# A four-layer convolution and state-space network on one core: its projections repacked as 128 + 64 columns, and the hand-planned instruction order made again with other costs

## The chip, the cores and the metric

The kernel runs on one core of a Trainium2 chip. A core has five engines that run side by side and meet only through semaphores: TensorE (PE, matrix products; its loads of stationary weights have a row of their own, PEld), VectorE (DVE), ScalarE (ACT), GpSimd (POOL) and SyncE (SP, which here only issues copies). Copies between the DRAM tensors and the on-chip tiles are carried out by 16 DMA engines that all queues share. The metric is the time of one execution in microseconds (us), lower is better: 9278.05 us is the median of three runs of the kernel before (9277.84, 9278.05 and 9299.97).

## What is computed

Sixty-four images of 96 channels and 28 x 28 pixels, all in float32, pass four layers. Layer 0 is an inverted residual block whose depthwise kernels and projection weights are mixed for each image out of four experts; layers 1 and 3 are plain inverted residual blocks; layer 2 is a selective state-space block on the four quarters of the image. The expansion goes from 96 to 576 channels, the projection back to 96.

```
# layer 0                                  (per image: rw = softmax weights of 4 experts)
out = silu(bn1(exp_w @ x))                 # 96 -> 576
out = silu(bn2(depthwise 5x5 (out, kern))) # kern = mix of 4 experts' kernels
out = out * sigmoid(squeeze-excite(out))
x   = x + bn3((mix of 4 experts' pw_w) @ out)   # 576 -> 96, the projection
# layers 1 and 3
out = relu(bn1(w1 @ x)); out = relu(bn2(depthwise 3x3 (out, wd)))
x   = x + bn3(w3 @ out)                    # 576 -> 96, the projection
# layer 2, for each quarter of the image
b = silu(dwconv3x3(p2(h))); b = four directional scans of b (16 states a channel); y = norm(b) * silu(p1(h))
x = x + y * gate(y)
```

## The kernel before, in words

All 64 images run through one program without loops; images are software-pipelined. In the slot of image t the scans of layer 2 run for image t (`mamba`, `scans`, `head`, `tail`), beside them the depthwise layers 1 of image t+1, 0 of image t+2 and 3 of image t-1 (`convs`), and the expansion of the next job.

**A convolution layer** has three parts. `expand` (L735, L765) multiplies the image with the expansion weights in eight products of 128 output channels by 392 pixels and one last pair of 64 channels; ACT takes each out of PSUM into a bordered tile (L719), and the ACT queue stores it in a DRAM tensor `ex` (L752, L778). `load` fetches it back on the SP queue into `rep`, each channel in several shifted rows (L791 with three copies for layer 0, L798 with four copies for layers 1 and 3), and fetches or builds the tap weights `wd` (L825 from DRAM, L598 on POOL). `depthwise` (L851) convolves: stationary weights of 32 columns in four column groups of the PE array, layer 0 with 96 rows, layers 1 and 3 with 64 rows and so two row groups at once; ACT takes each result into an `acc` tile (L861). There are nine `acc` tiles to a layer. A lane of `rep` and `acc` holds a channel together with the parity of the row, so that the 392 columns of an `acc` tile are half an image.

**The projection** (`project`) is what the change repacks. An `acc` tile g has 128 lanes: 64 channels, each for even rows (o = 0) and odd rows (o = 1). For each g and each parity one matmul with 96 output channels adds to one of two PSUM banks, with weights that are zero at the lanes of the other parity. That is 18 matmuls of 128 rows, 96 columns and 392 pixels a layer (L888). In float32 each of them is two records in the profile, and each record has its own weight load. Then DVE adds bank o and the bias to the rows of parity o of the image (L892, two instructions). For layer 0 the weights are made for each image: PE mixes the experts (L985), DVE multiplies in the gates (L1010, four instructions, 480 or 384 elements wide).

**The scans**: DVE multiplies (L1307) and scans forwards and backwards (L1312, L1317), POOL combines (L1264), ACT makes the decays (L1285) and copies `du` (L1295), PE collects (L1239).

**The order** of every engine's instructions is written by a planner, `Plan`. Each operation is entered with its engine, an assumed cost in us, what it reads and writes, and a due time: the slot's start `T * t` plus an offset, plus a correction from the table `DUE` for its kind. `Plan.run` then plays the program through with these assumed costs and issues, engine by engine, the operation that is ready and due first. On the chip only the order is kept; no due time is enforced. The planner knows which ACT function table is loaded (a change costs `TABLE`), and where it expects PE to lie idle it puts in products of zeros (L549, `idle`). Two things of it matter here: an operation is never issued more than `AHEAD` us before it is due, and a copy was assumed to arrive after its issue plus `land` (or a size by a rate) plus `LAND`. The copies' semaphores are eight in number and are handed out in turn, SP and ACT together: a copy waits until the one eight places earlier in the program has landed.

Of the kernel before, what the change touches and what calls it, by code (L numbers as in the profile page):

```python
# [15 lines left out]
P = 128  # L16
# [148 lines left out]
def pack_l1(ins, layer):  # L165
# [12 lines left out]
    out = np.zeros((4, 2, CB, 2, NG, C), np.float32)  # L178
    for o in range(2):
        out[:, o, :, o] = w3.reshape(4, 2, CB, NG, C)[:, o]  # L180
    p.add("w3", out.reshape(P, 2 * NG, C))
# [4 lines left out]
def pack_l2(ins):  # L186
# [41 lines left out]
PE, ACT, DVE, POOL, SP = "PE", "ACT", "DVE", "POOL", "SP"  # L228
EXP, PLUS, SILU = "exp", "plus", "silu"
# [11 lines left out]
    71, -2, 48, -17, 58, 181, 21, -12, 9, -37, -2, 21, 37, -23, 1, -16, 19, -12, 30, -17, 33, -40, 12, -8, -30, -60,  # L241
    -12, 9, 0, -16, 16, -56, 115, 47, -23, -9, 16, 45, -29, 63, -28, 34, 12, 35, 43, 2, -32, -7, 21, -7, 6, 14, 37,
    13, -22, 36, -19, 13, -27, 7, -23, -17, 130, -19, 113, 50, 16, 35, 28, 2, 22, 11, -45, 12, -30, 30, -30, -13, -6,
    -6, -12, -8, -7, 20, 24, 117, 11, 25, -20, 15, -13, 1, 51, 43, 29, 147, 47, 40, -10, -15, -7, 10, 30, -10, 20,
    129, 8, 11, 31,
# [17 lines left out]
class Plan:  # L263
# [4 lines left out]
    AHEAD = 45.0  # L268

    HOP = {PE: 1.0, DVE: 0.6, ACT: 0.4, POOL: 0.4, SP: 0.2}  # L270
    LAND = 0.7
    ALONE = 130e3
    RATE = 300e3
    TABLE = 1.28
    ANY_ORDER = ("ps", "gs")
    WARM, WINDOW = 0.7, 3.4
    GRACE = {PE: 0.3, ACT: 0.2, DVE: 0.25, POOL: 0.25, SP: 0.0}
# [10 lines left out]
    def op(self, engine, cost, fn, r=(), w=(), due=None, table=None, nbytes=0, after=(), land=None, lock=False):  # L288
        o = Op()
        o.engine, o.cost, o.fn, o.table, o.nbytes = engine, cost, fn, table, nbytes  # L290
        o.land, o.lock = land, lock or engine == POOL
        kind = self.k.kinds.setdefault((fn.__code__, self.tag), len(self.k.kinds))
        o.due = (self.due if due is None else due) + (DUE[kind] if kind < len(DUE) else 0.0)
# [39 lines left out]
    def run(self, start=0.0):  # L333
# [3 lines left out]
        table, dma, left, lock, ahead = None, start, len(self.ops), start, None  # L337
        used = []
# [18 lines left out]
        while left:  # L357
            best = None
            for e, q in queue.items():
                cands = []  # L360
                for o in q:
                    t = max(free[e], o.ready, o.due - self.AHEAD)
                    if o.lock:
                        t = max(t, lock)
                    if best and t > best[0] + 1.0:
                        continue
                    if o.allocs:
                        p = place(o)
                        if p is None:
                            continue  # L370
                        t = max(t, p)
                    cands.append((t, o))
# [3 lines left out]
                key = lambda c: (c[1].due + (8.0 if c[1].table and c[1].table != table else 0.0), c[1].n)  # L376
# [9 lines left out]
            if o.table and o.table != table:  # L386
                cost += self.TABLE
                table = o.table
            o.fill = 0.0
            if e == PE:  # L390
# [7 lines left out]
                used.append((t - o.fill, t + cost))  # L398
            free[e] = end = t + cost
            o.behind = None  # L400
# [7 lines left out]
            if o.nbytes:  # L408

                dma = max(dma, t + 0.5) + o.nbytes / self.RATE  # L410
                end = max(dma + 1.5, t + cost + (o.land or 2.0 + o.nbytes / self.ALONE)) + self.LAND
# [6 lines left out]
            for b in set(o.bufs):  # L418
                b.left -= 1
                b.end = max(b.end, end + 0.2)  # L420
            for d, data in o.out:
                d.wait -= 1
                if data:
                    d.ready = max(d.ready, end + (self.HOP[d.engine] if d.engine != e or o.nbytes else 0.0))
# [58 lines left out]
class Kernel:  # L483
    T = 145.0
# [13 lines left out]
        wp=(1, [P, 2, NG, C]),  # L498
# [90 lines left out]
    def fold_bn3(self, row, w3):  # L589

        k = w3.shape[1]
        self.nc.vector.tensor_tensor(w3, w3, row.rearrange("p (a o) -> p a o", a=1).to_broadcast([P, k, C]), ALU.mult)
# [12 lines left out]
    def setup(self, fold, banks):  # L605
# [22 lines left out]
        for layer, c in ((1, c1), (3, c3)):  # L628
# [4 lines left out]
            self.fold_bn3(self.row_of(banks, s3, eye, f"fold_row{layer}"), c("w3"))  # L633
# [75 lines left out]
    def expand(self, d):  # L709
# [17 lines left out]
        for t in range(4):  # L727
# [3 lines left out]
            for h in range(2):  # L731
                ps = pl.buf("ps")

                def mm(ps=ps, t=t, h=h):
# [4 lines left out]
                pl.op(PE, 0.72, mm, r=d["keys"], w=[ps], after=[("pad", i, h)])  # L739
                pl.op(  # L740
                    ACT, 0.68, lambda ps=ps, t=t, h=h, pad=pad: evict(pad[:, :, 1 + 7 * h : 8 + 7 * h, 2:30], ps, t),
# [4 lines left out]
            def send(t=t, pad=pad):  # L746
# [8 lines left out]
                ACT, 0.35, send,  # L755
                r=[("pad", i, 0), ("pad", i, 1)], w=[("ex", d["exkey"], t)], nbytes=524288, land=3.5,
# [23 lines left out]
        pl.op(PE, 0.81, mm, r=d["keys"], w=[ps], after=["hpad"])  # L780
        pl.op(ACT, 0.68, lambda: evict(pad[:, :, :, 2:30], ps, 4), r=[ps], w=["hpad"], table=d["table"])
        pl.op(ACT, 0.7, store, r=["hpad"], w=[("ex", d["exkey"], 4)], nbytes=230000, land=3.2)
# [19 lines left out]
    def load(self, d, u):  # L802
# [8 lines left out]
            SP, 0.32 * n, lambda: self.rows(d, rep, ch, sets),  # L811
            r=[("ex", d["exkey"], ch // P)], w=[rep], nbytes=n * CB * 4 * 1792, land=4.2 if sets == 2 else 2.8,
# [8 lines left out]
        if layer == 0:  # L821
            pl.op(POOL, 1.3, spread, r=[d["kern"]], w=[wd])
        else:
            pl.op(
                SP, 0.55, lambda: nc.sync.dma_start(wd()[:lanes, :TAPS], self.taps[layer][u][:lanes]),  # L825
                w=[wd], nbytes=lanes * TAPS * 4,
# [3 lines left out]
    def depthwise(self, d, u):  # L830
# [34 lines left out]
        pl.op(PE, 0.69 * k, mm, r=[rep, wd], w=[*banks, *accs])  # L865
        for h, (ps, acc) in enumerate(zip(banks, accs)):
            pl.op(
                ACT, 0.88 if sums else 0.68, lambda ps=ps, acc=acc, h=h: evict(ps, u if sums else 2 * u + h, acc),
# [3 lines left out]
    def project(self, d):  # L872
# [3 lines left out]
        if d["layer"] == 0:  # L876
            wp = self.squeeze_excite(d)
            terms = lambda o, g: (wp()[:, o, g], accs[g]())
        else:
            w3, wp = d["c"]("w3"), "none"  # L880
# [655 lines left out]
```

## Time and profile before

| what | before |
|---|---|
| median of 3 runs | 9278.05 us |
| the profiled execution | 9292.98 us (its span 9291.2 us) |
| granted TensorE clock, mean | 0.967 |
| PE, DVE, POOL, ACT busy | 96%, 84%, 73%, 68% of the span |
| products of zeros (L549) | 150 records, 71.6 us |
| ACT table loads, all lines | 1077 instructions in the program, 1283 ns each |
| all copies | 2030 MB, 218 GB/s, DMA engines 71% busy in mean |

The profile shows one execution. Its page gives each engine's busy time, groups of instructions by source line with their mean duration, and the idle time of the engine just before them with what ended it. A "busy" PE is a rough reading, since matmul records overlap each other; the distance from the start of one row of the timeline to the start of the next is the better measure of what a stretch of matmuls takes. The granted clock is the share of TensorE's full clock that was let through.

Once the pipeline is full, the images follow each other evenly. The routing product of layer 0 (L921) comes once an image; from its start at 555.84 us to that at 8897.88 us there are 59 images, 141.4 us each.

### The profile page before, as it was taken

The page shows a single profiled execution, that of the slowest core. Times are in us where ns is not written, and L with a number is a line of the kernel's source. Part 1 is how long each engine was busy: PE and PEld are TensorE (multiplying, and loading weights), DVE is VectorE, ACT ScalarE, POOL GpSimd, SP SyncE. Part 2 cuts the span into 40 slices and gives each one's busy share as a digit, 9 for nine tenths or more (in the row PEclk, how much of TensorE's full clock was granted, in tenths as well). Part 3 has the DMA queues.
Part 4 walks back from the last instruction along what each step waited for, and adds up shares of the span by engine and source line. Part 5 has one row for each costly group of instructions (what it writes and reads, how often), then busy time and mean ns, then how long its engine had stood idle before and what let it go on. Part 6 is the DMA issues. An engine that isn't in the chain of part 4 may idle for free. (4 is left out here: it accounts for less than half of the span.)

```text
span 9291.2 us, 198890 instructions
## 1 busy us (share of the span) xinstructions
PE 8881.7 (96%) x78114; PEld 4022.6 (43%) x78114; DVE 7772.6 (84%) x7806; ACT 6337.0 (68%) x10934; POOL 6774.3 (73%) x4445
## 2 busy tenths in 40 slices
PE   7899999999999999999999999999999999999997
PEld 3344444444444444444444444444444444444443
DVE  1888888888888888888888888888888888888887
ACT  3666767767667677667677676676776676776763
POOL 2777777777777777777777777777777777777775
PEclk9899999999999999999999999999999999999998
DMA  5677767777677677677677776776776776777773
GB/s 177 190 222 223 224 214 226 229 223 223 217 227 221 219 229 222 217 230 222 220 224 227 226 223 218 226 223 221 229 224 216 227 223 220 228 230 219 223 229 108
DMA packets 1068081, 2029.98 MB, mean 218 GB/s; under 512 B 118160, under 2 KB 894096, under 8 KB 1066768
## 3 DMA queue, kind: packets, MB, share of 16 engines
q1 hardware_dynamic: 814672, 1520.45, 54.3%
q10 hardware_dynamic: 252480, 496.79, 15.0%
q8 instruction: 625, 10.24, 0.5%
q14 instruction: 304, 2.49, 0.1%
HBM read 1499.83 MB, written 516.95 MB: 217 GB/s over the span
## 5 line engine op out<-in xcount | busy, mean ns | idle before, releaser
L851 PE MATMUL ps<-rep,wd 64*32 64x392 f32 (+1 forms) x50688 | 3668.3, 527 | 93.8 <-DMA rep<-ex 33.7
L1317 DVE TENSOR_TENSOR_SCAN g<-decay,b 128x788 f32<-128x788 f32 x1536 | 2755.3, 1794 | 292.9 <-ACT decay L1285 154.7
L1312 DVE TENSOR_TENSOR_SCAN h<-decay,b 128x788 f32<-128x788 f32 x1536 | 2722.0, 1772 | 0.0
L851 PEld LDWEIGHTS ps<-rep,wd 64*32 64x32 f32 (+1 forms) x50688 | 1413.1, 111 | 2007.6 <-issue 1724.9
L1264 POOL TENSOR_TENSOR yc<-h,g 128x784 f32<-128x784 f32 x768 | 1435.9, 1870 | 1098.5 <-DVE h L1312 526.2
L861 ACT ACTIVATE acc<-ps,l_bn2b,l_bn2s 128x392 f32<-128x392 f32 x1728 | 1124.5, 674 | 1439.1 <-PE ps L851 1415.8
L1307 DVE TENSOR_TENSOR b<-du,B 128x784 f32<-128x784 f32 x1536 | 1505.3, 980 | 689.4 <-ACT du L1295 622.0
L1264 POOL TENSOR_TENSOR g<-h,g 128x784 f32<-128x784 f32 x768 | 1425.5, 1856 | 813.6 <-DVE h L1312 813.2
L888 PE MATMUL ps<-acc,blob 128*96 128x392 f32 x4608 | 1603.3, 498 | 4.4
L1264 POOL TENSOR_TENSOR yc<-yc,C 128x784 f32<-128x784 f32 x768 | 1426.9, 1858 | 55.2
L1285 ACT ACTIVATE decay<-dd,A 128x784 f32<-128x784 f32 x1536 | 1372.4, 943 | 32.3 <-DVE h L1312 14.7
L1264 POOL TENSOR_TENSOR yc<-yc,g 128x784 f32<-128x784 f32 x768 | 1317.4, 1715 | 45.9
L735 PE MATMUL ps<-x,blob 96*128 96x392 f32 x3072 | 1176.9, 516 | 13.9 <-ACT border L719 8.3
L888 PEld LDWEIGHTS ps<-acc,blob 128*96 128x96 f32 x4608 | 726.4, 163 | 760.8 <-issue 669.3
L719 ACT ACTIVATE border<-ps,l_bn1b,l_bn1s 128x392 f32<-128x392 f32 x1536 | 975.5, 676 | 116.2 <-ACT border L719 75.5
L598 POOL TENSOR_TENSOR wd<-kern,blob 96x640 f32<-96x640 f32 x576 | 752.9, 1316 | 168.7 <-PE ps L851 145.7
L1285 ACT ACT_TABLE_LOAD x439 | 563.2, 1283 | 328.3 <-issue 114.2
L888 PE MATMUL ps<-acc,wp 128*96 128x392 f32 x2304 | 770.8, 493 | 0.6 <-ACT a L1182 0.6
L735 PEld LDWEIGHTS ps<-x,blob 96*128 96x128 f32 x3072 | 540.1, 191 | 527.2 <-ACT acc L861 79.4
L888 PEld LDWEIGHTS ps<-acc,wp 128*96 128x96 f32 x2304 | 376.0, 163 | 383.1 <-issue 373.0
L1295 ACT COPY du<-dd 128x392 f32<-128x392 f32 x768 | 374.2, 487 | 188.5 <-DVE b L1307 88.8
L1239 PE MATMUL y<-yc,blob 128*32 128x392 f32 x3072 | 398.4, 501 | 36.7 <-POOL yc L1264 36.7
(144 smaller groups left out, 6537.7 us busy)
## 6 DMA issues: line engine op xcount, KB each, us to landing
rep<-ex SPq DMA_DIRECT2D x3776, 224.0 KB, 4.1
ex<-border ACTq DMA_DIRECT2D x512, 480.0 KB, 4.4
dd<-ddd SPq DMA_DIRECT2D x384, 588.0 KB, 7.1
ex<-border ACTq DMA_DIRECT2D x256, 512.0 KB, 4.8
B<-bcd SPq DMA_DIRECT2D x256, 392.0 KB, 4.1
C<-bcd SPq DMA_DIRECT2D x256, 392.0 KB, 4.6
wd<-taps SPq DMA_DIRECT2D x512, 192.0 KB, 4.0
rep<-ex SPq DMA_DIRECT2D x512, 112.0 KB, 3.7
```

The source lines that it names most:

```text
L598: self.nc.gpsimd.tensor_tensor(out, taps.rearrange("k (n a) -> k n a", a=1).to_broadcast([k, n, cb]), mask.rearrange("k (a c) -> k a c", a ...
L719: nc.scalar.activation(dst, ps()[:, :HALF].rearrange("p (r o w) -> p o r w", o=2, w=28), d["func"], bias=bias[:, t : t + 1], scale=scale[: ...
L735: nc.tensor.matmul(ps()[:, :HALF], w1[:, t * P : t * P + P], x[:, h * HALF : (h + 1) * HALF], start=True, stop=True)
L851: nc.tensor.matmul(ps()[32 * b : 32 * b + 32, :HALF], wd()[64 * h : 64 * h + lanes, at : at + 2 * CB], rep()[64 * h : 64 * h + lanes, b, : ...
L861: nc.scalar.activation(acc(), ps()[:, :HALF], d["func"], bias=bias[:, at : at + 1], scale=scale[:, at : at + 1], **kw)
L888: nc.tensor.matmul(banks[o]()[:C, :HALF], w, a, start=(g == 0), stop=(g == NG - 1))
L1239: nc.tensor.matmul(y()[32 * j : 32 * j + 32, :HALF], c("sel"), ys[j]()[:, 2 * u : 2 * u + 2], start=(k == 0 and u == 0), stop=(k == 1 and ...
L1264: nc.gpsimd.tensor_tensor(*vs, op)
L1285: nc.scalar.activation(fs[:, :, u, :, :SEQ], d()[:, :2].rearrange("p o (i l) -> p o i l", i=2), AF.Exp, scale=self.A[:, at : at + 1],)
L1307: nc.vector.tensor_tensor(out, v, w, ALU.mult)
L1312: lambda h=h, ff=ff: nc.vector.tensor_tensor_scan(flat(h()), ff, b, 0.0, ALU.mult, ALU.add),
L1317: lambda g=g, ff=ff: nc.vector.tensor_tensor_scan(flat(g())[:, ::-1], ff[:, ::-1], b[:, ::-1], 0.0, ALU.mult, ALU.add),
```

## The change

It has two parts.

**The projection.** An image row of 96 output channels for both parities is 192 columns. They are laid as 128 + 64 in place of 96 + 96: the first matmul has all 96 channels of even rows and channels 64 to 95 of odd rows (128 columns, 392 pixels, bank 0); what is left, channels 0 to 63 of odd rows, is done by two matmuls of 64 columns and 196 pixels, side by side in the two column halves of the array (bank 1, one half of the pixels on each 64 partitions). For each g there are so three matmuls instead of two. They are issued in runs of three g: one operation of three full matmuls, one of six half-width ones. The additions to the image become four: two of 392 pixels on 96 and 32 partitions, two of 196 pixels on 64 partitions. The layer 0 weights are made in six multiplications instead of four.

**The order.** The planner's costs, due corrections and rules are other: `T` 134 for 145, `AHEAD` 500 for 45, all assumed costs new, at most eight copies under way in program order (`LANES`), copies of one operation issued one by one, a cost (`MODE`) for a change between full and tiled matmuls and a preference against it (`MODE_PEN`). No instruction outside the projections is of another shape or count, except for what the planner itself puts in: products of zeros and function table loads.

```diff
-    out = np.zeros((4, 2, CB, 2, NG, C), np.float32)
-    for o in range(2):
-        out[:, o, :, o] = w3.reshape(4, 2, CB, NG, C)[:, o]
-    p.add("w3", out.reshape(P, 2 * NG, C))
+    w3 = w3.reshape(4, 2, CB, NG, C)
+    out = np.zeros((4, 2, CB, NG, 2 * C), np.float32)
+    out[:, 0, :, :, :C] = w3[:, 0]
+    out[:, 1, :, :, C:P] = w3[:, 1, :, :, 64:]
+    out[:, 1, :, :, P:] = w3[:, 1, :, :, :64]
+    p.add("w3", out.reshape(P, NG, 2 * C))
...
-    AHEAD = 45.0
+    AHEAD = 500.0
+    LAG = {PE: 0.0, DVE: tick(0.1), ACT: tick(0.1), POOL: tick(0.05), SP: 0.0}
+    LANES = 8
+    TABLE, MODE = tick(1.28), tick(0.1)
+    MODE_PEN = 0.5
...
+                    if o.nbytes:
+                        t = max(t, landed[-self.LANES])
...
+            if o.nbytes:
+                step, s, lands = tick(cost / o.copies), t, []
+                wait = 2.0 + tick(o.nbytes / o.copies / self.ALONE) if o.land is None else tick(o.land)
+                for i in range(o.copies):
+                    s = max(s, landed[i - self.LANES])
+                    dma = max(dma, s + 0.5) + tick(o.nbytes / o.copies / self.RATE)
+                    s += step
+                    lands.append(max(dma + 1.5, s + wait) + self.LAND)
+                landed = (landed + lands)[-self.LANES :]
+                cost, arrival = s - t, max(lands)
...
-    T = 145.0
+    T = 134.0
...
         pl.op(
-            SP, 0.32 * n, lambda: self.rows(d, rep, ch, sets),
-            r=[("ex", d["exkey"], ch // P)], w=[rep], nbytes=n * CB * 4 * 1792, land=4.2 if sets == 2 else 2.8,
+            SP, 0.45 * (3 if layer == 0 else 4), lambda: self.rows(d, rep, ch, sets),
+            r=[("ex", d["exkey"], ch // P)], w=[rep], nbytes=n * CB * 4 * 1792 * (0.92 if layer == 0 else 0.8 if sets == 2 else 1.4), land=2.6,
+            copies=3 if layer == 0 else 4,
         )
...
-        def mm(lo):
+        def mm(half, lo):
             for g in range(lo, lo + 3):
-                for o in range(2):
-                    w, a = terms(o, g)
-                    nc.tensor.matmul(banks[o]()[:C, :HALF], w, a, start=(g == 0), stop=(g == NG - 1))
+                w, a, kw = weights()[:, g], accs[g](), dict(start=(g == 0), stop=(g == NG - 1))
+                if half == 0:
+                    nc.tensor.matmul(banks[0]()[:, :HALF], w[:, :P], a, **kw)
+                    continue
+                for h in range(2):
+                    nc.tensor.matmul(
+                        banks[1]()[64 * h : 64 * h + 64, :SEQ], w[:, P:], a[:, h * SEQ : h * SEQ + SEQ], **kw
+                    )
...
+        def first():
+            add(xs(0), banks[0]()[:C, :HALF], 0, C)
+            add(xs(1)[64:], banks[0]()[C:, :HALF], 64, C)
+
+        def second():
+            for h in range(2):
+                add(xs(1)[:64, 7 * h : 7 * h + 7], banks[1]()[64 * h : 64 * h + 64, :SEQ], 0, 64)
...
         for lo in range(0, NG, 3):
-            pl.op(PE, 0.67 * 6, lambda lo=lo: mm(lo), r=[*(accs[lo : lo + 3] if lo else accs), wp], w=banks)
-        for o in range(2):
-            pl.op(DVE, 0.65, lambda o=o: add(o), r=[banks[o], *d["keys"]], w=d["keys"])
+            ready = [*(accs[lo : lo + 3] if lo else accs), wp]
+            pl.op(PE, 1.97, lambda lo=lo: mm(0, lo), r=ready, w=[banks[0]])
+            pl.op(PE, 1.27, lambda lo=lo: mm(1, lo), r=ready, w=[banks[1]], table=TILED)
+        pl.op(DVE, 1.3, first, r=[banks[0], *d["keys"]], w=d["keys"])
+        pl.op(DVE, 0.78, second, r=[banks[1], *d["keys"]], w=d["keys"])
```

## The prediction, made before the changed kernel had run

> **What bounds the kernel now.** I read the page first, then the busy time of the engines in the even part of the run, then PE's timeline through one image, then who waits for whom.
>
> ```profile
> span 9291.2 us, 198890 instructions
> PE 8881.7 (96%) x78114; PEld 4022.6 (43%) x78114; DVE 7772.6 (84%) x7806; ACT 6337.0 (68%) x10934; POOL 6774.3 (73%) x4445
> L888 PE MATMUL ps<-acc,blob 128*96 128x392 f32 x4608 | 1603.3, 498 | 4.4
> L888 PE MATMUL ps<-acc,wp 128*96 128x392 f32 x2304 | 770.8, 493 | 0.6 <-ACT a L1182 0.6
> 2000.00:8000.00 6000.00, 5820.32 (x51805) 2634.06 (x51796) 5139.29 (x5131) 4209.28 (x7267) 4480.36 (x2932) 0.97 0.71 224
> ```
>
> The last line's columns are PE, PEld, DVE, ACT, POOL busy, then granted clock, DMA share and GB/s, from 2000 to 8000 us. At 141.4 us an image that stretch holds 42.4 images, so an image has 4.2 us of PE idle (180 / 42.4) against 20.3 of DVE (861 / 42.4); DVE is busy 121.2 us an image, ACT 99.3, POOL 105.7. PE sets the pace. Rows of its timeline (start, length, what, records, idle before) give prices:
>
> ```profile
> 4016.65 2.17 PE L1157 MATMUL ps<-p,blob 128*32 128x196 f32 x36
> 4018.75 0.90 PE L1178 MATMUL ps<-hn,blob 96*96 96x392 f32 x2
> ...
> 4020.34 12.02 PE L888 MATMUL ps<-acc,wp 128*96 128x392 f32 x36
> 4032.28 4.28 PE L851 MATMUL ps<-rep,wd 64*32 64x392 f32 x96
> 4036.49 2.90 PE L735 MATMUL ps<-x,blob 96*128 96x392 f32 x8
> 4039.32 1.52 PE L1239 MATMUL y<-yc,blob 128*32 128x392 f32 x12
> 4040.77 2.90 PE L735 MATMUL ps<-x,blob 96*128 96x392 f32 x8
> 4045.60 0.33 PE L1091 MATMUL ps<-gs,blob 96*96 96x2 f32 x2 [1.92 <-ACT border L719]
> ...
> 4049.16 6.66 PE L851 MATMUL ps<-rep,wd 64*32 64x392 f32 x72
> 4056.67 2.25 PE L851 MATMUL ps<-rep,wd 64*32 64x392 f32 x48 [0.85 <-ACT acc L861]
> ...
> 4087.53 0.88 PE L765 MATMUL ps<-x,blob 96*64 96x392 f32 x4
> 4088.34 2.96 PE L735 MATMUL ps<-x,blob 96*128 96x392 f32 x8
> ```
>
> Start to start, the projection's 36 records take 11.94 us (4020.34 to 4032.28): 0.332 us a record of 392 pixels, whatever its width up to 128 columns. Side by side in column groups records share that time: L1157's 36, three abreast on 196 pixels, take 2.10 us. An image has also one stall. ACT is behind with the expansion's evictions, PE lies idle 1.92 us, and then L851's 72 records take 6.66 us where 48 take 2.25. The clock shows why:
>
> ```profile
> 4045.00:4050.00 5.00, 3.90 (x23) 2.24 (x31) 4.79 (x4) 3.62 (x10) 1.36 (x1) 0.69 0.73 246
> 4050.00:4058.00 8.00, 7.15 (x104) 3.80 (x95) 7.73 (x6) 5.61 (x11) 6.72 (x8) 0.77 0.75 248
> ```
>
> The granted clock falls to 0.69 and 0.77, which costs 0.31 x 3.90 + 0.23 x 7.15 = 2.9 us of these PE spans, on top of the idle time.
>
> **The projection, priced.** An image has three. Removed: 3 x 36 records, 3 x 11.94 = 35.8 us. Added in full: 54 records x 0.332 = 17.9 us; that they have 128 columns and not 96 costs nothing, since L735 with 128 columns keeps the same step. Added in halves: 27 g x 2 passes = 54 passes of two records abreast, 64 columns and 196 pixels. The trace has no such pass. From below: L1157's twelve passes in 2.10 us, less 0.12 for its entry (below), 0.165 us each. From above, with concurrency: L765, two abreast of the right width but 392 pixels, takes 0.81 us for two passes, 0.15 over 2 x 0.332; 0.10 of that is the entry, and the other 0.045 seems to be a weight load that doesn't hide; paid in every pass it makes 0.21 us. Without concurrency it would be 0.33. I take 0.165, since L735 shows such an extra as well and only once: its records start 434 ns apart the first time after an entry and 329 ns apart from then on. That makes 54 x 0.165 = 8.9 us, with 11.3 kept as the upper value. Sum: 17.9 + 8.9 - 35.8 = -9.0 us an image.
>
> A rule of the Trainium skill speaks against that. "TensorE: Matmul & The Clock Gate", Part 3, "The mechanism", says that a weight load overlaps running matmuls only where the row group differs; column halves share all rows. L1157 has three column tiles on the same 128 rows, and its passes still take only the streaming time, so here the row and the rule differ. By the rule each pass would pay its loads (142 ns is the mean of L765's load): 54 x 0.142 = 7.7 us an image, and the sum would shrink to -1.3.
>
> **Entries.** A change of array shape costs. L735's eight records take 2.83 us where 8 x 0.332 = 2.65: 0.18 for an entry of 128 columns. L1239's twelve records, four passes, take 1.45, 0.12 over: an entry of 32 columns; L765's 0.15 is one of 64. In the compiled order an image has 49 entries before and 54 after: the full shape 21 then 18, 64 columns 3 then 9, 64 rows by 32 columns 6 then 8, the rest equal. That is -3 x 0.18 + 6 x 0.15 + 2 x 0.12 = +0.6 us. (Of an image's three projections, one has its six runs of halves merged to one stretch, one to two, one to three; the nine full matmuls stand together in all three.)
>
> **Products of zeros.** 75 then 265 in the program; in the even part none before, three an image after, 426 columns wide. L549's six records of 476 columns near the end take 2.51 us (9239.92 to 9242.43), so three products, six records, of 426 take 2.2 us. They stand in front of a `head`'s shifted products, where PE is to wait. If PE idles there anyhow they cost nothing; if it doesn't, +2.2. I count them in full, and count off the clock dip of 2.9 us that such filling can avoid, since the stall above was the even part's dip: -0.7 together. The two ends: -2.9 (filled idle time, no dip) and +2.2 (all extra, dip as before).
>
> **Other engines.** DVE per projection: before 2 x 0.616 us (L892's mean), after 2 x 0.616 + 2 x 0.404 (L1396, 96 x 196, is the nearest row), +0.81, three times 2.4 us. The weights' two extra multiplications: L1010 runs 590 ns in the middle and 100 ns per 96 elements between its two widths, so some 0.15 us is fixed: +0.3. DVE gets 121.2 + 2.7 = 123.9 us an image; hidden as long as an image takes clearly more, and 2.7 if DVE becomes the bound. Bank 0 is now given up after two DVE instructions of 1.23 us, bank 1 after 0.81, so PSUM is not held longer. ACT: 1077 table loads become 903, 2.7 an image x 1.283 = 3.5 us less; the stall above came from ACT's queue, so this helps PE there, but I count it inside the dip. POOL and the number of copies on SP and ACT stay.
>
> **The new order** moves almost every instruction, and PE, ACT and SP queues are all rearranged, so its waits can't be read off one edit. What the trace says of the old one's weakness: ACT's queue is held by copies.
>
> ```profile
> 4050.28 1.75 ACTq L778 DMA_DIRECT2D ex<-hborder  x2
> 4052.12 0.49 ACT L1295 COPY du<-dd 128x392 f32<-128x392 f32 x1 [1.87 <-DMA rep<-ex]
> ```
>
> Two issues take 1.75 us where one takes 0.52, waiting for a `rep` copy eight places earlier; behind them stands `du`, and DVE's largest wait is for `du`. These waits come to 87 us in the run. The new plan knows them; I give no credit, since PE is the bound.
>
> **The sum.** 141.4 - 9.0 + 0.6 - 0.7 = 132.3 us an image. The profiled span is 64 x 141.4 + 241, and I leave the 241 us of filling, setup and emptying as they are: 64 x 132.3 + 241 = 8708. The profiled execution took 9293.0 with a median of 9278.1, 15 less, and a span 2 us shorter: 8708 + 2 - 15 = 8695 us.
>
> **Rivals.** (1) DVE takes over. Its 123.9 us of work plus the waits that aren't PE's fault: of its 20.3 us idle, 5.8 are for PE's results (L892 191 us, L1344 116, L996 64 in the run, over 64). 123.9 + 14.5 = 138.4 us, 64 x 138.4 + 241 - 13 = 9086. For it:
>
> ```profile
> DVE b L1307 <- ACT du L1295: 622.0, 202, 14.1
> ```
>
> 9.7 us an image. Against it: the longest of these is 14.1 us, one lump after a `head` that itself waits for PE.
>
> (2) Slower than before: PE waits at L851 for `rep`. The planner's new costs let a load arrive 0.45 x 3 + 2.6 + 0.7 = 4.65 us after its first issue (layer 0) or 5.1 us (four copies); in the trace the medians from first issue to last landing are 6.1 and 6.5 us. A plan that relies on it puts PE 1.4 us too early, for 19 loads up to 27 us an image. It decides the sign from 0.48 us a load on average (9.1 / 19). With 0.8 us a load, 15.2 us: 147.5 an image, 9668. Against it: three `rep` tiles let loads run ahead, and PE waited
>
> ```profile
> PE ps L851 <- DMA rep<-ex: 33.7, 21, 5.8
> ```
>
> only, with an order that had been made without any limit on copies.
>
> (3) The halves don't run abreast: 54 x (0.33 - 0.165) = +8.9, 141.2 an image, 9265: no change. L765's two abreast in 0.81 us speak against it.
>
> **How the numbers follow.** The forecast case, PE stays the bound: its best is 132.3 - 2.2 (zeros in idle time) with a further 1.2 of idle gone, 128.9, 8477; its worst 132.3 + 2.4 (passes of 0.21) + 2.9 (dip stays) = 137.6, 9035. I give it 0.77, with its own 8-in-10 range 8530 to 8900. DVE takes over 0.12, slower through loads 0.08, no change 0.03. The range, 8520 to 8960, leaves out the two last cases and the upper half of the DVE case. About 0.3% (28 us) is what a measurement can tell from no change. Faster 0.77 + 0.12 = 0.89, same 0.03, slower 0.08.
>
> **What would show it.** Right: L888's successor with 3456 full records at 0.33 us steps and half-width stretches of 36 records in some 3.1 us (18 passes and an entry); images 130 to 135 us apart; granted clock above 0.98; DVE at 92 to 95%. Wrong: stretches of 36 in 4 us or more; PE waits for `rep` of hundreds of us; DVE waits for `du` as large as before with PE idle beside them. The prediction falls if an image takes over 137 us or under 129.

## The result, and the profile after

The changed kernel takes 9390.9 us (median of 4 runs, 9379.2 to 9416.2), the kernel before 9278.0 beside it (4 runs, 9277.8 to 9300.0): a ratio of 1.0119, interval 1.0093 to 1.0146. It is 1.2% slower. The forecast was 8695 us, and the range, 8520 to 8960, does not hold the result.

The page of the changed kernel, with engine totals and, from its list of the costliest groups, the two halves of the projection:

```profile
span 9377.4 us, 207032 instructions
PE 8630.0 (92%) x81950; PEld 4005.5 (43%) x81950; DVE 7981.7 (85%) x8322; ACT 6169.2 (66%) x10760; POOL 6786.4 (72%) x4445
L920 PE MATMUL ps<-acc,blob 128*128 128x392 f32 x2304 | 792.6, 498 | 36.8 <-ACT cz L1427 36.8
L923 PE MATMUL ps<-acc,blob 128*64 128x196 f32 x4608 | 433.3, 338 | 0.0
```

and the busy time from 2000 to 8000 us, columns as before:

```profile
2000.00:8000.00 6000.00, 5609.48 (x53833) 2601.46 (x53832) 5237.90 (x5437) 4050.67 (x7077) 4450.47 (x2908) 0.96 0.70 222
```

PE has less to do, 5609 us instead of 5820, and stands idle for more, 390.5 instead of 179.7. The mean granted clock of the run fell from 0.967 to 0.954. So work was saved and then lost in waiting. To see how much of each, I split an image's time in three. The distance between images comes from the second routing product (L921 before, L969 after), 59 images as in the section on the kernel before. Idle is the part of 2000 to 8000 us in which no matmul runs. "Clock" is half of PE's busy time in the stretches for which the trace gives a granted clock of one half. What remains is work at full clock.

| us an image | before | after | forecast | difference, after to before |
|---|---|---|---|---|
| from image to image | 141.4 | 142.5 | 132.3 | +1.1 |
| work at full clock | 133.4 | 127.7 | 127.2 | -5.7 |
| idle | 4.2 | 9.3 | 4.2 | +5.0 |
| clock | 3.7 | 5.5 | 0.8 | +1.8 |

(The differences are those of the unrounded figures. The forecast's column is its own terms: 133.4 - 9.0 + 0.6 + 2.2 of zeros, idle as before, the dip of 2.9 taken off the clock.)

The place is easy to find. PE's largest wait is a new one, 53 times in the 64 images, and SP and DVE have one at the same place; the waits of the changed kernel (in total, times, longest):

```profile
PE ps L884 <- DMA wd<-taps: 218.3, 53, 5.6
SPq L858 <- DMA ddd<-dd: 360.6, 61, 7.9
DVE rw L956 <- DMA x<-x_dram: 234.7, 60, 5.0
```

PE's timeline through one of these images; L884 is the depthwise product that was L851:

```profile
5788.38 3.21 PE L923 MATMUL ps<-acc,blob 128*64 128x196 f32 x36
5791.51 1.58 PE L767 MATMUL ps<-x,blob 96*128 96x392 f32 x4
...
5797.66 6.19 PE L920 MATMUL ps<-acc,blob 128*128 128x392 f32 x18 [0.59 <-ACT cz L1427]
5803.78 0.33 PE L1431 MATMUL ps<-cz,blob 12*96 12x2 f32 x2
...
5815.62 2.82 PE L884 MATMUL ps<-rep,wd 64*32 64x392 f32 x48 [1.40 <-ACT a L1229]
5823.26 3.77 PE L884 MATMUL ps<-rep,wd 64*32 64x392 f32 x48 [4.82 <-DMA wd<-taps]
```

The projection runs as priced: 18 full records in 6.12 us and 36 of half width in 3.13 (start to start). Then PE lies idle 1.40 and 4.82 us in 10 us, and the 48 records behind that take 3.77 us where the same 48 take 2.25 elsewhere: the granted clock has dropped, to 0.76 in the mean from 5820 to 5827 us. What the taps waited for stands on SP's timeline, and beside it ACT's:

```profile
5812.74 3.13 SPq L830 DMA_DIRECT2D rep<-ex  x4
5820.55 0.33 SPq L858 DMA_DIRECT2D wd<-taps  x1
5820.97 0.38 SPq L1501 DMA_DIRECT2D x<-x_dram  x1
```

```profile
5816.22 0.32 ACTq L1256 DMA_DIRECT2D ddd<-dd  x1
```

SP is through with `rep` at 5815.87 and issues nothing for 4.7 us, though the taps lie ready in DRAM. ACT issued the store of `ddd` in that time, and from 5808 to 5830 us the trace gives 4.3 us from its issue to its landing: 5816.22 + 4.3 = 5820.5, just when SP goes on. The load of the taps waits for a store that carries nothing it needs. The reload of `x`, queued behind it on SP, is held too, and with it DVE (L956, 4.47 us idle at 5824.43). The chain of waits of another image, from 8795 to 8820 us, goes the same way:

```profile
8805.87 0.58 ACT a L1229
8806.45 0.63 ACT acc L894 x2
8807.08 4.53 DMA ddd<-dd
8811.61 0.02 issue
8811.63 2.51 DMA wd<-taps
8814.14 0.14 issue
8814.28 4.18 PE ps L884 x48
```

The cause lies between the plan and the program. The planner counts "at most eight copies under way, in program order", SP's and ACT's together. But it fixes only the order within each engine. How the two queues interleave in the compiled program, and thereby which copy takes which of the eight semaphores, is left to the compiler. Counted in the compiled program of the changed kernel, 2018 of 7356 places hold a copy of the other queue than planned. ACT's are usually 4 to 6 places early. An image has two stores of `ddd`, one for each half of it; the first is mostly 4 places early, the second 12 to 13 early in 61 of the 64 images. So a taps load comes to stand eight places behind the second store, in 60 images, though ACT issues that store only later; in the plan a reload of `ddd` itself stands there.

### The profile page after: what moved, and what is told of

It is laid out like the page before. It is cut to its first block, busy times and chain, and to the rows that moved or that the text cites. A ratio compares the mean times of both kernels' runs of the same rounds, so it can differ in the third digit from the quotient of the medians.

```text
span 9377.4 us, 207032 instructions
## 1 busy us (share of the span) xinstructions
PE 8630.0 (92%) x81950; PEld 4005.5 (43%) x81950; DVE 7981.7 (85%) x8322; ACT 6169.2 (66%) x10760; POOL 6786.4 (72%) x4445
## 5 line engine op out<-in xcount | busy, mean ns | idle before, releaser
L884 PE MATMUL ps<-rep,wd 64*32 64x392 f32 (+1 forms) x50688 | 3647.1, 518 | 392.3 <-DMA wd<-taps 218.3
L1359 DVE TENSOR_TENSOR_SCAN h<-decay,b 128x788 f32<-128x788 f32 x1536 | 2757.6, 1795 | 288.7 <-ACT decay L1332 138.9
L1364 DVE TENSOR_TENSOR_SCAN g<-decay,b 128x788 f32<-128x788 f32 x1536 | 2721.1, 1772 | 1.9
L884 PEld LDWEIGHTS ps<-rep,wd 64*32 64x32 f32 (+1 forms) x50688 | 1282.6, 109 | 2324.0 <-issue 1951.9
L767 PE MATMUL ps<-x,blob 96*128 96x392 f32 x3072 | 1288.1, 537 | 149.7 <-ACT border L751 74.3
L751 ACT ACTIVATE border<-ps,l_bn1b,l_bn1s 128x392 f32<-128x392 f32 x1536 | 1002.2, 677 | 229.9 <-PE ps L767 206.1
L628 POOL TENSOR_TENSOR wd<-kern,blob 96x640 f32<-96x640 f32 x576 | 751.2, 1317 | 135.9 <-PE ps L884 61.8
L920 PE MATMUL ps<-acc,blob 128*128 128x392 f32 x2304 | 792.6, 498 | 36.8 <-ACT cz L1427 36.8
L930 DVE SCALAR_TENSOR_TENSOR x<-ps,l_bn3b,x 64x196 f32<-64x196 f32 (+2 forms) x768 | 396.0, 516 | 220.4 <-PE ps L920 205.2
L920 PEld LDWEIGHTS ps<-acc,blob 128*128 128x128 f32 x2304 | 427.3, 190 | 330.7 <-ACT cz L1427 42.6
L923 PE MATMUL ps<-acc,blob 128*64 128x196 f32 x4608 | 433.3, 338 | 0.0
L920 PE MATMUL ps<-acc,wp 128*128 128x392 f32 x1152 | 396.3, 498 | 0.0
```

Of the source, the lines that this page charges most:

```text
L628: self.nc.gpsimd.tensor_tensor(out, taps.rearrange("k (n a) -> k n a", a=1).to_broadcast([k, n, cb]), mask.rearrange("k (a c) -> k a c", a ...
L751: nc.scalar.activation(dst, ps()[:, :HALF].rearrange("p (r o w) -> p o r w", o=2, w=28), d["func"], bias=bias[:, t : t + 1], scale=scale[: ...
L767: nc.tensor.matmul(ps()[:, :HALF], w1[:, t * P : t * P + P], x[:, h * HALF : (h + 1) * HALF], start=True, stop=True)
L884: nc.tensor.matmul(ps()[32 * b : 32 * b + 32, :HALF], wd()[64 * h : 64 * h + lanes, at : at + 2 * CB], rep()[64 * h : 64 * h + lanes, b, : ...
L920: nc.tensor.matmul(banks[0]()[:, :HALF], w[:, :P], a, **kw)
L923: nc.tensor.matmul(banks[1]()[64 * h : 64 * h + 64, :SEQ], w[:, P:], a[:, h * SEQ : h * SEQ + SEQ], **kw)
```

## The experiments

Each kernel was run beside the kernel before on the same chip, 4 runs each: e1 to e4, e5 to e8 and e9 to e11 each on one chip, where the kernel before took 9282, 9288 and 9295 us. Between these groups the ratio is therefore safer than the time. "Idle", "clock" and "work" are us an image, as above, from the profiled run.

| run | us | ratio to before, interval | image | idle | clock | work |
|---|---|---|---|---|---|---|
| before | 9278.0 | | 141.4 | 4.2 | 3.7 | 133.4 |
| after | 9390.9 | 1.0093 to 1.0146 | 142.5 | 9.3 | 5.5 | 127.7 |
| e1 after, copies as planned | 9044.7 | 0.9728 to 0.9757 | 137.3 | 5.4 | 4.0 | 127.9 |
| e2 old order, packed | 9610.2 | 1.0338 to 1.0369 | 146.6 | 10.1 | 9.0 | 127.5 |
| e3 new order, not packed | 9710.5 | 1.0438 to 1.0473 | 148.0 | 7.9 | 4.2 | 135.9 |
| e4 before, copies as planned | 9215.8 | 0.9915 to 0.9945 | 140.2 | 3.7 | 3.4 | 133.1 |
| e5 after, `ddd` stores as planned | 9122.0 | 0.9798 to 0.9855 | 137.8 | 6.2 | 3.7 | 127.9 |
| e6 e3, copies as planned | 9416.7 | 1.0125 to 1.0160 | 143.0 | 4.3 | 2.6 | 136.1 |
| e7 e2, copies as planned | 9555.4 | 1.0271 to 1.0328 | 145.8 | 10.3 | 8.0 | 127.4 |
| e8 e1 without zeros | 9087.5 | 0.9763 to 0.9802 | 138.2 | 6.6 | 6.2 | 125.4 |
| e9 e1, `ddd` stores left free | 9397.6 | 1.0091 to 1.0135 | 142.9 | 7.1 | 8.2 | 127.7 |
| e10 e1, more zeros | 9032.3 | 0.9706 to 0.9753 | 136.4 | 5.1 | 3.0 | 128.3 |
| e11 e1, zeros before the squeeze | 9029.7 | 0.9684 to 0.9747 | 137.1 | 5.3 | 2.1 | 129.7 |

### e1 and e4: all copies in the planned order

In `Plan.emit` each copy is ordered behind the copy planned just before it, on whichever queue. No semaphore wait is added for data; the compiled program only takes over the plan's interleaving.

```diff
+            if o.nbytes:
+                if last.get("copy"):
+                    self.k.tc.add_manual_dep(
+                        i,
+                        last["copy"].name,
+                        mybir.DependencyInfo(mybir.DependencyClass.NoSync, mybir.DependencyReason.DATA),
+                        reason="lanes",
+                    )
+                last["copy"] = i
```

The changed kernel with it:

> The changed kernel with every engine's own order as it is; only the copies of SP and ACT are also held, in the program, in the order in which the planner placed them, so that the copy eight places earlier is the one that the planner counted on. In the changed kernel 2018 of 7356 places hold a copy of the other queue than planned; ACT's store of ddd stands 12 to 13 places early, and the load of taps behind it waits for it. Theory 'copies' (the new order loses its gain because copies wait for a copy that was planned after them): PE's wait of 5 us an image at the depthwise matmuls for taps and the clock dip behind it (1.8 us) go; 142.5 - 6.9 = 135.6 us an image, 9391 - 60 x 6.9 = 8980 (8900 to 9060), PE's wait for wd<-taps from 218 us to under 40. Theory 'tight costs' (the plan is late everywhere since its costs are too small, the copies are where it shows): another wait takes its place, 9250 or more.

Measured: 9044.7 us, 346 us less than the change alone and 2.6% less than the kernel before. The wait for the taps is all but gone:

```profile
PE ps L893 <- DMA wd<-taps: 24.7, 31, 1.9
```

(Lines are 9 higher in this kernel.) SP's queue at the same place of an image shows the taps directly behind `rep`, and the store follows on ACT at 5626.71, where the taps no longer wait for it:

```profile
5619.88 2.52 SPq L839 DMA_DIRECT2D rep<-ex  x4
5622.45 0.59 SPq L867 DMA_DIRECT2D wd<-taps  x1
5623.14 1.14 SPq L1510 DMA_DIRECT2D x<-x_dram  x1
```

The kernel before with the same edit:

> The kernel before with its copies held in their planned order as in the first run. The old planner knew nothing of eight semaphores, so its order isn't made for them. Theory 'copies': nothing to gain, 9278 within 90 either way. Rival 'the pinned order is better in itself': 9150 or less.

Measured: 9215.8 us, 62 us or 0.7% less, within the 90 us that had been given. The compiled program of the kernel before departs from its plan about as often (with the setup 1916 of 7385 places hold a copy of the other queue, 2024 in the changed kernel). But the old plan was made without the eight places, and following it gains little.

### e5 and e9: the stores of `ddd` against all other copies

In e5 only the stores of `ddd` are held behind the copy planned before them, in e9 every copy but these. The condition picks both stores of an image, the one that stood 12 to 13 places early and the one that stood 4 early. In e9 the chain breaks at each of them: the next copy is tied to the store, not to the copy planned before the store.

```diff
-                if last.get("copy"):
+                if last.get("copy") and o.engine == ACT and o.nbytes == 451584:
```

> The changed kernel (9390.9 us); of all copies only ACT's store of ddd (L1256, 61 or so of them, which stands 12 to 13 places ahead of its planned place) is held behind the copy that was planned before it. All other copies stay where the compiled program had them. Theory 'one store': nearly all that the pinned order of all copies recovered (346 us) comes from this one store, since it was the one whose landing the taps load waited for: 9040 to 9130 us, and PE's wait for the taps falls from 218 us to under 60. Rival 'many copies': the gain is spread over the other 1900 places that differ: 9230 to 9390 us.

Measured: 9122.0 us. 269 of the 346 us, 78%, come back by the two stores of an image, and the wait for the taps falls from 218.3 us to 38.9:

```profile
PE ps L893 <- DMA wd<-taps: 38.9, 41, 2.4
```

The theory holds. Of the two stores the second is the one that the taps load had stood behind; what the first contributes was not measured apart.

```diff
-                if last.get("copy"):
+                if last.get("copy") and not (o.engine == ACT and o.nbytes == 451584):
```

> The changed kernel with every copy held to the planned sequence except ACT's store of ddd, which is free to stand early. It is the other half of the run that held this store alone (9122.0 us; all copies held: 9044.7 us; none: 9390.9 us). If the two halves add, what the store alone recovered (269 us) is missing here: 9390.9 - 346 + 269 = 9314 us, 9270 to 9350. Rival: the store's wait comes only together with the other early copies, then most of the gain stays: 9050 to 9150 us, and PE's wait for the taps is small without holding the store.

Measured: 9397.6 us. Both expectations were wrong: the two halves do not add. With the stores free, holding the others brings nothing; with the stores held it brings another 77 us. The waits and SP's timeline of e9 show why:

```profile
SPq L839 <- DMA ddd<-dd: 267.2, 62, 6.4
```

```profile
5693.79 5.47 SPq L839 DMA_DIRECT2D rep<-ex  x4
5699.31 0.58 SPq L867 DMA_DIRECT2D wd<-taps  x1
```

The store of the second half still stands 8 places early in the compiled program, the store of `bc` behind it 7 early, and the SP copies between are 1 or 2 late. So e9 is not the exact other half of e5. Eight places behind the store now stands a `rep` load, which waits instead of the taps load, 5.47 us for four issues that take 2.48 in e1. The taps stand behind it in the queue all the same. PE waits less than in the changed kernel (7.1 us idle an image against 9.3) but loses 8.2 us to the clock against 5.5:

```profile
5692.84 2.84 PE L893 MATMUL ps<-rep,wd 64*32 64x392 f32 x48 [1.39 <-ACT a L1238]
5696.83 2.28 PE L893 MATMUL ps<-rep,wd 64*32 64x392 f32 x48 [1.15 <-ACT acc L903]
...
5701.83 2.44 PE L893 MATMUL ps<-rep,wd 64*32 64x392 f32 x24 [1.06 <-DMA wd<-taps]
...
5704.37 4.29 PE L776 MATMUL ps<-x,blob 96*128 96x392 f32 x6
...
5709.10 8.59 PE L929 MATMUL ps<-acc,blob 128*128 128x392 f32 x18
```

Three gaps of 1.1 to 1.4 us, none long by itself, and the next products run at half clock (0.67 in the mean from 5701.5 to 5717 us): six records take 4.29 us (2.24 in e1), a projection's 18 take 8.59 (6.19).

### e2 and e7: the packing in the old order

The kernel before with the projection's part of the diff only: a group of three is one operation of full and half-width products, at the old cost; the two additions become four at the old costs.

```diff
-            pl.op(PE, 0.67 * 6, lambda lo=lo: mm(lo), r=[*(accs[lo : lo + 3] if lo else accs), wp], w=banks)
+            pl.op(PE, 0.67 * 6, lambda lo=lo: (mm(0, lo), mm(1, lo)), r=[*(accs[lo : lo + 3] if lo else accs), wp], w=banks)
...
-            pl.op(DVE, 0.65, lambda o=o: add(o), r=[banks[o], *d["keys"]], w=d["keys"])
+            pl.op(DVE, 0.65, lambda o=o: second() if o else first(), r=[banks[o], *d["keys"]], w=d["keys"])
```

> The kernel before with the packing alone: every run of three g is one planned operation of the old cost, three full and six half-width matmuls in it, and the two additions are as before two operations; so every engine's order is that of the kernel before. Theory 'copies' and theory 'tight costs' alike (the packing pays, the order loses): 27 x 2 half-width passes and 54 full records in place of 108 records, less 0.6 for more changes of shape (here 6 more a projection are possible, up to 2.5 us an image): 9.0 - 2.5 = 6.5 to 8.4 us an image, 9278 - 64 x 6.5 = 8860 down to 8740. Rival 'the packing does not pay' (the additions on DVE or the weights' loads take back what PE gains): 9250 or more.

Measured: 9610.2 us, 3.5% slower than the kernel before; a clear miss. Work fell by 5.9 us an image, but idle rose by 5.9 and the clock's loss by 5.3. PE's waits and a part of its timeline in e2 (L739 is the expansion, L901 the additions to `x`):

```profile
PE ps L739 <- DVE x L901: 188.9, 62, 3.5
PE ps L1107 <- ACT border L723: 180.7, 61, 3.6
```

```profile
5687.64 2.24 PE L891 MATMUL ps<-acc,blob 128*128 128x392 f32 x6
5689.81 1.22 PE L894 MATMUL ps<-acc,blob 128*64 128x196 f32 x12
5690.96 0.93 PE L739 MATMUL ps<-x,blob 96*128 96x392 f32 x2
5693.09 0.93 PE L739 MATMUL ps<-x,blob 96*128 96x392 f32 x2 [1.21 <-DVE rw L954]
5697.13 1.65 PE L739 MATMUL ps<-x,blob 96*128 96x392 f32 x2 [3.11 <-DVE x L901]
```

and DVE's additions there, with those of the kernel before at the same place of an image:

```profile
5695.73 2.16 DVE L901 SCALAR_TENSOR_TENSOR x<-ps,l_bn3b,x 96x392 f32<-96x392 f32 x4
```

```profile
5660.41 1.15 DVE L892 SCALAR_TENSOR_TENSOR x<-ps,l_bn3b,x 96x392 f32<-96x392 f32 x2
```

The old order issues the next expansion right behind the projection, and the expansion needs the sum in `x`. In the kernel before the additions start 0.2 us after the projection's end (5660.24). In e2 they start 4.7 us after it (5691.03), because in DVE's order, which is the old one, other work stands before them; then they take 2.16 us in four instructions, not 1.15 in two. PE waits there, 188.9 us in the run, where the expansion of the kernel before (L735) had 13.9 us of idle from all causes. It waits as long again for ACT's evictions (L723), but these 180.7 us were 118.7 already in the kernel before (L1091). How the waits and the clock hang together was not taken apart.

> The old order with the packed projection (9610.2 us) and all copies held to the planned sequence. Theory: what makes this mixture slow is not copies but that the next expansion and the next projection stand directly behind the additions to x, so PE waits for DVE and its clock falls. Then the pinning gives no more than the 62 us that it gave the kernel before: 9500 to 9620 us, with PE's wait for x at the expansion as large as before (189 us). Rival: it was copies that came late here too; then it falls under the old order without the packing, to 8900 to 9250 us.

Measured: 9555.4 us, 55 less than e2, about what the edit gave the kernel before (62), with the wait for `x` unchanged (189.3 us). The order of the copies is not the cause there.

### e3 and e6: the new order without the packing

The changed kernel with the projection as before; the planner and its costs stay as they are, so the order is that of the changed kernel.

```diff
-                w, a, kw = weights()[:, g], accs[g](), dict(start=(g == 0), stop=(g == NG - 1))
...
+                w, a = terms(half, g)
+                nc.tensor.matmul(banks[half]()[:C, :HALF], w, a, start=(g == 0), stop=(g == NG - 1))
```

> The changed kernel with the projection unpacked again (96 + 96 columns, two additions) inside the same planned operations, so that every engine's order is that of the changed kernel. If the packing gains in the new order what it was priced at, this is slower by up to 8.4 us an image, less what PE's idle time at the waits takes up (4.8 us at the taps' wait): 9391 + 64 x 3.6 to 9391 + 64 x 8.4, that is 9620 to 9930. Rival 'the new order is bound by something else than PE': 9391 within 60.

Measured: 9710.5 us, 5.0 us an image more than the changed kernel and inside the range expected.

> The new order with all copies held to the planned sequence (9044.7 us) and the projection as before, 36 records of 96 columns and 392 pixels each time. Theory: where less of PE's time is lost to waits, the packing shows more of its price than the 5.0 us an image that it showed with the copies unpinned (9710.5 less 9390.9, over 64). Priced alone it is 8.4 us an image (9.0 less 0.6 for entries), so 9044.7 + 64 x 8.4 = 9582 at most; I expect 9480 to 9590. Rival: PE's longer projection is again hidden in part by waits that it covers, and the packing stays at 5 us an image: 9330 to 9400.

Measured: 9416.7 us, 372 more than e1 or 5.8 us an image: above the rival's 5 but under what I expected. The split explains it. Without the packing PE's work is 8.2 us an image more in both pairs (135.9 against 127.7, 136.1 against 127.9), the priced 8.4. But the longer projection covers waits: idle is 1.1 us less than in e1 and the clock's loss 1.4 less.

Read across, these runs show that neither part of the change pays by itself. Without the packing the new order is slower than the old one, by 432 us as compiled (e3 against before) and by 201 us with the copies held (e6 against e4); the held pair differs by 2.8 us an image, and its work by 3.0, of which e8 puts 2.5 down to the products of zeros. In the old order the packing is slower too (e2, e7). As compiled, both parts together are slower by 113 us; with the copies held, they are faster than the held old kernel by 171 us (e1 against e4).

### e8, e10, e11: the products of zeros

e8 makes `idle` return at once, so no zeros are issued:

> The new order with all copies held to the planned sequence (9044.7 us), without the products of zeros (idle issues nothing; 2.3 us of PE an image). Theory 'on the path': the zeros are placed where the planner sees PE idle, and on the chip PE is behind the plan there, so they only delay what stands behind them: 64 x 2.3 = 147 us less, 8890 to 8960 us. Rival 'idle anyhow': PE waits in their place and the time stays, 9030 to 9060 us. Rival 'clock': without them the clock falls behind that gap and it becomes slower, 9070 to 9200 us.

Measured: 9087.5 us. They take 2.5 us of work an image; without them the clock loses 2.2 more and idle 1.2. So they earn what they cost and 0.9 us more, 43 us in the run: the rival "clock".

e10 raises `WARM` from 0.7 to 1.0. e11 puts two products of zeros of 480 columns, `self.idle(ps(), 1.6)`, at the head of `squeeze`:

> All copies as planned (9044.7 us) and the planner's share of PE time that products of zeros fill up to raised from 0.7 to 1.0 (WARM); the order of all else is the same. Two more places an image get zeros, in front of the last halves of a projection and of the second small product of the gate. Theory 'clock': products of zeros earn more than they take (without any of them it was 9087.5 us), so more of them give 9000 to 9040 us. Rival 'measure is full': the two places are short waits that cost no clock, and the zeros delay what stands behind: 9050 to 9120 us.

> All copies as planned (9044.7 us) and two more products of zeros an image, 480 columns each, 1.6 us of PE, directly before the squeeze-excite products (L1017), in front of the stretch where L1042's 16 records took 3.05 us at half clock instead of 1.66. Theory: the half clock there follows from PE doing little in the 18 one-column products and the wait before them; zeros in front of them keep the clock, 1.5 us an image or more is gained and 1.6 paid: 9000 to 9060 us with the clock above 0.975. Rival: the small products are what lowers the clock, whatever stands before; then 1.6 us an image are added, 9120 to 9160 us with the same clock.

Measured: 9032.3 and 9029.7 us. The four runs of each (9001 to 9053, 8996 to 9050) overlap those of e1 (9029 to 9055), and so do the intervals of the ratios, so neither is told apart from it. That also leaves e10 between its theory and its rival; e11's rival, 9120 us or more, is out. The clock did what was expected in e11, 0.976 in the run's mean against 0.964. The 16 records of L1042 took 3.05 us in e1:

```profile
5696.79 1.69 PE L1017 MATMUL ps<-sums,blob 128*96 128x1 f32 x18 [0.34 <-ACT acc L903]
...
5701.06 3.05 PE L1042 MATMUL ps<-w,mix 128*32 128x480 f32 x16
```

and 1.66 in e11 (one line lower there), behind the zeros:

```profile
5690.48 1.88 PE L588 MATMUL ps<-zero 128*128 128x480 f32 x4 [0.29 <-ACT acc L903]
5692.20 1.61 PE L1018 MATMUL ps<-sums,blob 128*96 128x1 f32 x18
...
5696.18 1.66 PE L1043 MATMUL ps<-w,mix 128*32 128x480 f32 x16
```

Over the whole run the median record of this product takes 847 ns in e1 and 566 in e11. 1.9 us of clock were gained an image and 1.8 of work paid.

## Why the prediction was wrong, step by step

**The projection, -9.0, and the entries, +0.6: right.** The changed work is -8.2 us an image in two pairs (e3 to after, e6 to e1) against -8.4. A stretch of 36 half-width records takes 3.13 us where 3.1 was forecast, so the halves run abreast and a pass takes (3.13 - 0.15) / 18 = 0.166 us, the value taken, not the upper 0.21. Rival (3) is out, and so is the skill's rule on weight loads in "TensorE: Matmul & The Clock Gate" (Part 3, "The mechanism"), by which the sum would have been -1.3: here the measurement decides. In e2 the saving is only 5.9, since there three and three alternate: three times 2.17 + 1.15 us make 9.96 a projection, against 6.12 + 3.13 = 9.25 in one piece. That is 0.7 us a projection and 2.1 an image, an estimate from these rows; the gap is 2.3. Grouping by shape was worth what the entries were priced at: alternating adds four entries a projection, two at 0.18 and two at 0.15, 0.66 us together.

**Zeros and dip, "-0.7 together": wrong by 5.0.** The zeros came as counted (+2.5 by e8, 2.2 priced). But the dip did not vanish; the clock's loss rose by 1.8 us instead of falling by 2.9. The dip I had looked at was one place; the new order made others. One is the mixing of the experts' weights, whose median record took 566 ns before (L985) and 847 after (L1033); another stands behind the wait for the taps.

**"The new plan knows them; I give no credit, since PE is the bound", and the waits carried over unchanged: the step that failed, by 5.0 us of idle and, through the clock, part of the line above.** I took 4.2 us of idle an image as a constant of the kernel. It is a property of the order, and the order was made anew. The new plan did know the eight places, but the program that was compiled from it did not keep them, and I had not compared the two. e1 shows the size: with the places kept, idle falls by 3.9 us an image and the clock's loss by 1.5, together 5.4 of the 6.8 us that the change had added to them. e5 shows that most of it hangs on the stores of `ddd`: held to their places they bring 78% of the time back. In e9, with these stores free, nothing comes back.

**Rival (2) had the right line and the wrong copy.** PE does wait at the depthwise product, but for `wd`, 218.3 us, while its waits for `rep` are 24.9 us in the run. Not a landing time planned too short, as the rival had it, but an issue held back by a wait for a semaphore. Its point of decision, 9.1 us an image, came about in another way: 6.8 of idle and clock and 2.5 of zeros against 8.2 saved make +1.1.

**DVE, +2.7 us an image: about right.** Its busy time rose from 121.1 to 124.4, by 3.3. Rival (1), DVE as the bound, was never reached: e1 runs at 137.3 us an image with DVE busy 124.2. ACT fell by 3.0 us, where 3.5 had been worked out from the table loads; no gain from that can be seen in PE's waits.

**What is left in e1.** It is 5.0 us an image above the forecast: 0.7 of work (127.9 against 127.2), 1.2 of idle and 3.2 of clock. The rest of the idle time is in short waits, the largest 84.0 us in the run for ACT (`a`, L1238), 59.5 for DVE. They were not taken apart further.

## What to carry to other kernels

Price the work of an edit from rows, but treat idle time and clock as belonging to the order: when the order is made anew, both have to be found again, and they can eat more than the edit saves. Where a planner counts a shared resource, compare the program that results with the plan, instruction by instruction; here holding the stores of `ddd`, one of them a dozen places early, brought back 269 us. And a shorter product pays only if the next work in its queue does not wait for what another engine makes of its result (e2).

## What had not been expected of the hardware

The clock can fall at gaps much shorter than I had thought. In e9 three gaps of 1.39, 1.15 and 1.06 us within 11 us, PE working in between, were followed by 10.2 us at half clock; in e1, with 1.40 and 0.24 us at the same place, the clock stayed at 1.00. In the stretch before L1042 in e1 there was only a wait of 0.34 us, then 18 one-column products in 1.69 us, four dense records and a few more small products. The Trainium skill, "TensorE: Matmul & The Clock Gate" ("Why this matters for your kernels"), asks for no idle gaps over about 3 us; these runs show that keeping under it is not enough, and e11 that a little dense work ahead of the sparse stretch can avoid the fall. What decides between e9 and e1 was not found.

A copy can be held by one that it has nothing to do with, and holds its whole queue. In the kernel before I had read this only on ACT's queue (87 us), and overlooked more of it on SP's: the taps load (L825) stood there behind the store of `bc`, which it does not use either.

```profile
SPq L825 <- DMA bcd<-bc: 440.0, 61, 11.1
PE ps L851 <- DMA wd<-taps: 13.9, 12, 3.4
```

It waited 440.0 us in the run and cost PE at most 13.9. In the changed kernel a wait of 360.6 us on SP cost PE 218.3. So the size of a wait in a copy queue does not tell its price; how soon the next engine needs the copy does.

"DMA: Bandwidth & Descriptors" in the Trainium skill ("Anatomy of one DMA — SWDGE (gpsimd) path") says that a wait for a semaphore is kept by the issuing sequencer, before the copy is handed over. The section is on copies that GpSimd issues; SP's 4.7 us without an issue fit the same account.
